# Nodes left in their own order, a written order across engines, and a paced gather stream, in a four-layer graph network

## The chip, the cores and the metric

The kernel runs on one core of a Trainium2 chip. The core has five engines with an instruction queue each: PE (TensorE, matrix products and transposes into PSUM), DVE (VectorE, elementwise work, reductions, sorting steps), ACT (ScalarE, activations and copies), POOL (GpSimd, which here issues indirect DMAs, that is gathers and scatters by a list of row numbers) and SP (SyncE, which issues plain DMAs). They run side by side and wait for each other through semaphores.

The metric is the device time of one execution in microseconds (us). The kernel before took 2909.86 us, the median of 11 runs (2902.86 to 2919.98).

## What is computed

There are 16 graphs of 1024 nodes with 64 features. `adj` is a weighted adjacency matrix with about nine entries per row and the diagonal. Four layers follow each other, each on `h = relu(layernorm(x))` and each added to `x`. The first is a product with `adj` and a weight; the second is a two-layer perceptron, a product with `adj` and a GRU cell; the third is a Chebyshev stack of degree 3, that is two products with `adj`. The fourth needs the work that the change is about:

```python
adj_ = jnp.where(eye[None], 1.0, adj)                 # the node itself counts
nb = (adj_ > 0) & (~eye)[None]
m = nb.sum(-1)
skip = jnp.where(m > 10, (m + 1) // 2, 1)             # nodes with over 10 neighbours
removed = nb & do_dil & ((rank + 1) % skip == 0)      # drop every skip-th neighbour
valid = where(removed | removed.T, 0, adj_) > 0
sv = sort(where(valid, x[neighbour], big), axis=neighbour)
agg = sum over (0.25, 0.5, 0.75) of weight * interpolated quantile of sv, per feature
y = relu((x + agg) @ W1 + b1) @ W2 + b2
```

So for every node and every feature the values of the node and its kept neighbours are sorted, and quantiles of the sorted values are mixed.

## The kernel before, in words

**Lists.** Per graph, `lists` loads eight row tiles of the adjacency (128 x 1024 numbers, L340). DVE turns each into keys (L342), finds the neighbours' keys with MAX8 and MATCH_REPLACE8 (L345 to L350) and writes up to 24 neighbour numbers per node, the count and the two dropped neighbours into `pay`, a row of everything that is known of a node. PE transposes the same row tiles (L356), ACT copies them out of PSUM (L357) into `AT`, which the three matrix layers use.

**Layers.** `layers` runs the first three layers of one graph as one chain: layer norm (DVE L450 and L451, ACT L455, L457 and L463), products with `AT` (L472), small products (L483), the GRU (L518 to L538). The last norm writes `h` into `pay` (L463); then SP stores `h` and the two dropped neighbours as rows of a DRAM table (L721).

**Classes.** Four graphs make a group of 4096 nodes. `positions` ranks the group's nodes by neighbour count, and 32 scatters on POOL (L318) write their `pay` rows to DRAM in that order. The sorted nodes are cut into ten classes, `CLASSES = ((1, 25), (3, 13), ..., (5, 6))`: so many tiles of 128 nodes with at most so many values each. `quantile_class` loads a class's rows (L600), and POOL gathers one neighbour for 128 nodes with each instruction (L606). DVE marks dropped neighbours (L611 to L618), adds a large number to them (L621), sorts by min and max over two buffers (L663, L665) and weighs the sorted places (L673). PE sums them (L680) and computes the perceptron (L689 to L700), DVE finishes the result (L703, L705), and POOL scatters it to `out`, a scatter for each tile (L318).

**Order.** `run` issues, for each graph of a group, the lists, the layers, the store and a quarter of the ten classes of the group before. After the last group its ten classes follow alone. Each engine keeps its queue's order. The tables' unused halves are filled once with large numbers by 64 stores from ACT (L301).

Of the kernel before, what the change touches and what calls it, by code (L numbers as in the profile page):

```python
# [22 lines left out]
P = 128  # L23
# [13 lines left out]
GG = 4  # L37
GT = GG * NT
LIST = 24
BINS = LIST + 1  # L40
FAR = 2000.0
STRIDE = 2 * N
# [3 lines left out]
for _n in (1, 1, 1, 1, LIST, C, 2, C):  # L46
    ROW.append(ROW[-1] + _n)
SELF, TO, COUNT, MASK, IDX, H, DROPS, XS, W = ROW

CLASSES = ((1, 25), (3, 13), (3, 11), (3, 11), (4, 10), (2, 9), (3, 9), (4, 8), (4, 7), (5, 6))  # L50
BIG = 1e30

# [103 lines left out]
def fast_constants():  # L156
# [6 lines left out]
        "bins": np.broadcast_to((BINS - 1 - np.arange(BINS))[None, :], (P, BINS)),  # L163
        "ordinal": np.broadcast_to(1 + np.arange(LIST)[None, :], (P, LIST)),
    }
    kmax = max(n for _, n in CLASSES)
    cap = np.array([n for tiles, n in CLASSES for _ in range(tiles)])
# [4 lines left out]
        "shift": np.broadcast_to(P * np.arange(NT)[None, :], (P, NT)),  # L172
        "place": np.broadcast_to(np.arange(kmax)[None, :], (P, kmax)),
        "taus": np.broadcast_to(np.array([TAUS[0], TAUS[1], TAUS[1], TAUS[2]])[None, :], (P, 4)),

        "room": np.broadcast_to(P * np.array([(cap - 1 >= BINS - 1 - b).sum() for b in range(BINS)])[None, :],
                                (P, BINS)),
    }
# [8 lines left out]
    return tables  # L187


class Fast:  # L190
# [4 lines left out]
    def __init__(self, tc, half, whole, weights):  # L195
# [19 lines left out]
        self.ones16 = fixed("ones16", [P, GT * BINS], F16)  # L215
# [7 lines left out]

        self.aug = fixed("aug", [C + 1, N], F32)
        nc.vector.memset(self.aug[C:C + 1, :], 1.0)

        with tc.tile_pool(name="fsetup", bufs=1) as sp, \
# [12 lines left out]
            self.w2a = fixed("w2a", [C + 1, C], F32)  # L240
            nc.sync.dma_start(self.w2a[:C, :], W2)
            nc.sync.dma_start(self.w2a[C:C + 1, :], b2[None, :])
            self.wca = fixed("wca", [C + 1, C], F32)
            nc.sync.dma_start(self.wca[:C, :], Wc)
            nc.sync.dma_start(self.wca[C:C + 1, :], bc[None, :])
# [35 lines left out]
            tmax = max(t for t, _ in CLASSES)  # L281
            self.mb2r = fixed("mb2r", [1, tmax, C], F32)
            nc.sync.dma_start(self.mb2r, mb2[None, None, :].to_broadcast([1, tmax, C]))

        self.p1 = pool("f1", 1)
        self.p2 = pool("f2", 2)
        self.p3 = pool("f3", 3)
        self.pp = pool("fpay", GG + 2)
        self.ps = pool("fps", 1, space=PSUM)
        self.ps2 = pool("fps2", 2, space=PSUM)  # L290
        self.ps3 = pool("fps3", 3, space=PSUM)
        self.pd = pool("fd", 2, space=DRAM)
        void = self.p1.tile([P, C + 2], F32, name="void")
        nc.vector.memset(void, BIG)
        fixed_d = pool("fdconst", 1, space=DRAM)
        self.tables = []
        for i in range(2):
            table = fixed_d.tile([GG * STRIDE, C + 2], F32, name=f"table{i}")
            for s in range(GG * 2 * NT):
                if s // NT % 2:  # L300
                    nc.scalar.dma_start(table[s * P:(s + 1) * P, :], void)  # L301
            self.tables.append(table)
        self.overs = 0
        self.written = []

    def feature_bank(self, rows=C):
        return self.ps3.tile([P, 512], F32, name="fm")[0:rows, :]

    def after(self, ins, earlier):

        self.tc.add_manual_dep(ins.ins, earlier.ins.name,
                               mybir.DependencyInfo(mybir.DependencyClass.Sync, mybir.DependencyReason.DATA),
                               reason="rows of a scatter")

    def scatter(self, out, rows, at, done):


        ins = self.nc.gpsimd.indirect_dma_start(  # L318
            out=out, out_offset=bass.IndirectOffsetOnAxis(ap=at, axis=0), in_=rows, in_offset=None)
        if done:  # L320
            self.tc.declare_no_dep(ins.ins, done[-1].ins, reason="rows of their own")
        done.append(ins)
# [6 lines left out]
    def lists(self, b, g, adj, nodemask, pay, d):  # L329
# [3 lines left out]
        nc, p1, p2 = self.nc, self.p1, self.p2  # L333
        halves = [self.p3.tile([P, NT, 512], F32, name="AT") for _ in range(2)]
        cand = p2.tile([P, NT, NB], F16, name="cand")
        L = p2.tile([P, NT, LIST], F16, name="L")
        sums = p2.tile([P, NT], F32, name="sums")
        for t in range(NT):
            A = self.p2.tile([P, N], F32, name="A")
            nc.sync.dma_start(A, adj[b, t * P:(t + 1) * P, :])  # L340
            key = p2.tile([P, N], F16, name="key")
            nc.vector.scalar_tensor_tensor(key, A, 0.0, self.keys[:, (NT - 1 - t) * P:(NT - 1 - t) * P + N],  # L342
                                           op0=ALU.is_gt, op1=ALU.mult, accum_out=sums[:, t:t + 1])
            for s in range(NT):
                nc.vector.max(out=cand[:, t, 8 * s:8 * s + 8], in_=key[:, s * P:(s + 1) * P])  # L345
            for s in range(LIST // 8):
                top = L[:, t, 8 * s:8 * s + 8]
                nc.vector.max(out=top, in_=cand[:, t, :])
                if s < LIST // 8 - 1:
                    nc.vector.match_replace(out=cand[:, t, :], in_to_replace=top,  # L350
                                            in_values=cand[:, t, :], imm_value=0.0)
            for h in range(2):
                tp = self.ps2.tile([P, 4, P], F32, name="tp")
                for q in range(4):
                    j = 4 * h + q
                    nc.tensor.transpose(tp[:, q, :], A[:, j * P:(j + 1) * P], self.ident)  # L356
                nc.scalar.activation(halves[t // 4][:, 4 * h:4 * h + 4, (t % 4) * P:(t % 4 + 1) * P], tp, AF.Copy)  # L357

        mu8 = p1.tile([NT, P], U8, name="mu8")
        nc.sync.dma_start(mu8, nodemask[b, :].rearrange("(t p) -> t p", p=P))  # L360
        mf = p1.tile([NT, P], F32, name="mf")
        nc.vector.tensor_copy(mf, mu8)
        mps = self.ps.tile([P, NT], F32, name="mps", tag="nm")
        nc.tensor.transpose(mps, mf, self.ident[:NT, :NT])
        nc.vector.tensor_copy(pay[:, :, MASK], mps)
        nc.vector.tensor_scalar(pay[:, :, SELF], self.node, float(b * N), None, op0=ALU.add)
        nc.vector.tensor_scalar(pay[:, :, TO].bitcast(I32), self.node, float(b * N), None, op0=ALU.add)

        def small(name, n=1):
            return p2.tile([P, NT, n] if n > 1 else [P, NT], F32, name=name)  # L370

        def wide(name, n=1):
            return p1.tile([P, NT, n, LIST] if n > 1 else [P, NT, LIST], F16, name=name)

        some = wide("some")
        nc.vector.tensor_scalar(some, L, 0.0, None, op0=ALU.is_gt)
        cnt = small("cnt")
        nc.vector.tensor_reduce(cnt, some, axis=AX.X, op=ALU.add)
        found = small("found")
        nc.vector.tensor_reduce(found, L, axis=AX.X, op=ALU.add)  # L380
        nc.vector.tensor_sub(found, sums, found)
        nc.vector.tensor_reduce(self.over_column(), found, axis=AX.X, op=ALU.max)

        skip = small("skip")
        nc.vector.tensor_scalar(skip, cnt, 0.5, 0.25, op0=ALU.mult, op1=ALU.add)
        nc.vector.tensor_scalar(skip, skip, MAGIC, MAGIC, op0=ALU.add, op1=ALU.subtract)
        dil = small("dil")
        nc.vector.scalar_tensor_tensor(dil, cnt, 10.0, pay[:, :, MASK], op0=ALU.is_gt, op1=ALU.mult)  # L390
        nc.vector.scalar_tensor_tensor(skip, skip, FAR / 2, dil, op0=ALU.subtract, op1=ALU.mult)
        at = p2.tile([P, NT, 3], F16, name="at3")
        nc.vector.tensor_scalar(at[:, :, 0], skip, FAR / 2, None, op0=ALU.add)
        nc.vector.tensor_scalar(at[:, :, 1], skip, 2.0, FAR, op0=ALU.mult, op1=ALU.add)
        nc.vector.tensor_scalar(at[:, :, 2], skip, 2.0, FAR - 1.0, op0=ALU.mult, op1=ALU.add)
        hit = wide("hit", 3)
        for i in range(3):
            nc.vector.tensor_tensor(hit[:, :, i, :], self.ordinal[:, None, :].to_broadcast([P, NT, LIST]),
                                    at[:, :, i:i + 1].to_broadcast([P, NT, LIST]), op=ALU.is_equal)
# [33 lines left out]
    def layers(self, b, x, halves, pay):  # L433
# [6 lines left out]
        def nodes(name):  # L440
            return p2.tile([P, NT, C], F32, name=name)
# [153 lines left out]
    def quantile_class(self, s0, T, n, rows, placed, table, out):  # L595
# [5 lines left out]
        for ins in placed:  # L601
            self.after(load, ins)
# [763 lines left out]
```

## Time and profile before

| | |
|---|---|
| median of 11 runs | 2909.86 us |
| the profiled execution | 2905.68 us |
| its span in the profile | 2903.9 us |
| mean granted PE clock | 0.683 |
| gathers L606: instructions, busy, mean | 1092, 1150.8 us, 1054 ns |
| scatters to rows L318: instructions, busy, mean | 128, 147.7 us, 1154 ns |
| scatters to out L318: instructions, busy, mean | 128, 162.3 us, 1268 ns |
| a gather's issue to landing, min / median / max | 2.3 / 2.5 / 6.6 us |
| key L342: instructions, busy | 128, 154.6 us |
| sort L665 and L663, the three largest groups, busy | 362.5, 215.5, 53.8 us |
| mask L621, weigh L673, busy | 78.9, 85.0 us |
| product passes with AT, L472 | 2048, busy 559.2 us |
| last gather starts, span ends | 2855.9, 2903.9 us |

The span is the time from the first to the last recorded instruction; the run is a little longer. The page of the profile gives each engine's busy time, a strip of 40 slices with the busy share in tenths, and groups of instructions by line and tile. The view of the waits says, for each engine and line, for whom it stood idle and for how long. The timeline lists instructions with start, duration, engine, line, operation and tiles, and in brackets the idle time before them. The windows give busy time for stretches of the span. An instruction on POOL here is the issue of a DMA: its duration is the time POOL needs to describe 128 row transfers, and the data land later. Durations of DVE instructions that follow each other overlap a little, so the time from start to start is shorter than the mean duration.

### The profile page before, as it was taken

The numbers are of one execution on the slowest core, as the hardware profiler recorded it, in microseconds if no ns is written. First come the engines' busy times: TensorE is split into PE (matmuls) and PEld (weight loads), VectorE is DVE, ScalarE is ACT, GpSimd is POOL, SyncE is SP. The second block draws the span as 40 slices with busy tenths as digits, with TensorE's granted clock in tenths as the row PEclk, the third lists the DMA queues.
The fourth block names the chain that finished last, engine by engine and source line by source line (L and its number), as shares of the span: only waits on it lengthen the run. The fifth ranks groups of instructions, "written<-read, shape, count | busy, mean of one in ns | idle before, by whom it ended". The sixth has DMA issues, their size and how long they took to land. (4 is left out here: it accounts for less than half of the span.)

```text
span 2903.9 us, 22669 instructions
## 1 busy us (share of the span) xinstructions
PE 1484.4 (51%) x6173; PEld 789.9 (27%) x6173; DVE 1547.7 (53%) x5020; ACT 807.3 (28%) x2410; POOL 1461.0 (50%) x1352
## 2 busy tenths in 40 slices
PE   2676766556466574656546646575566412121122
PEld 1333233233223232333213232343232202010111
DVE  4555255475756663676657372667564414544342
ACT  2344354242323242424214232333333100000000
POOL 0000004753644557727546657645646776565764
PEclk9777777667667576767666766676787655555555
DMA  4122012130303131302113131303111111111110
GB/s 123 37 66 66 17 49 96 32 86 16 89 16 89 21 91 44 85 20 67 45 20 92 25 92 42 90 16 87 24 31 32 41 39 23 25 28 21 30 31 16
DMA packets 125605, 142.18 MB, mean 49 GB/s; under 512 B 68766, under 2 KB 87390, under 8 KB 125470
## 3 DMA queue, kind: packets, MB, share of 16 engines
q1 hardware_dynamic: 54142, 82.05, 9.2%
q0 software_dynamic: 45184, 51.54, 8.8%
q10 hardware_dynamic: 26144, 7.07, 1.1%
q8 instruction: 51, 0.84, 0.1%
q14 instruction: 84, 0.69, 0.1%
HBM read 119.51 MB, written 21.04 MB: 48 GB/s over the span
## 5 line engine op out<-in xcount | busy, mean ns | idle before, releaser
L606 POOL DMA_INDIRECT G<-table,PS x1092 | 1150.8, 1054 | 493.9 <-issue 325.4
L680 PE MATMUL q<-buf,c 128*128 128x192 f32 (+4 forms) x696 | 204.2, 464 | 636.3 <-DVE buf L673 636.1
L318 POOL DMA_INDIRECT rows<-pay,at x128 | 147.7, 1154 | 511.3 <-ACT sq L455 469.1
L318 POOL DMA_INDIRECT out<-yo,PS x128 | 162.3, 1268 | 428.0 <-DVE yo L705 303.4
L665 DVE TENSOR_TENSOR buf<-buf 128x576 f32<-128x576 f32 (+11 forms) x552 | 362.5, 681 | 5.1 <-ACT buf L620 0.5
L472 PE MATMUL fm<-AT,h 128*64 128x512 f32 x1024 | 277.2, 694 | 153.6 <-ACT h L463 153.4
L680 PEld LDWEIGHTS q<-buf,c 128*128 128x128 f32 x696 | 162.6, 279 | 681.1 <-DVE buf L673 602.3
L611 DVE TENSOR_TENSOR hits<-G,PS 128x48 f32<-128x48 f32 (+5 forms) x40 | 8.7, 216 | 632.3 <-DMA G<-table,PS 627.3
L472 PE MATMUL fm<-AT,m 128*64 128x512 f32 x1024 | 282.0, 698 | 44.2 <-DVE m L550 37.4
L356 PE MATMUL tp<-c,A 128*128 128x128 f32 x1024 | 205.8, 364 | 178.4 <-DMA A<-in_adj 94.3
L345 DVE MAX8 cand<-key 128x8 f16<-128x128 f16 x1024 | 224.7, 273 | 0.1
L356 PEld LDWEIGHTS tp<-c,A 128*128 128x128 f32 x1024 | 163.5, 189 | 224.9 <-ACT AT L357 106.6
L357 ACT ACTIVATE AT<-tp 128x512 f32<-128x512 f32 x256 | 146.6, 592 | 260.2 <-PE fm L472 110.8
L665 DVE TENSOR_TENSOR buf<-buf,buf 128x384 f32<-128x384 f32 (+9 forms) x460 | 215.5, 497 | 2.3
L455 ACT ACTIVATE sq<-X,st 128x64 f32<-128x64 f32 x384 | 128.2, 336 | 247.9 <-DVE st L451 246.8
L342 DVE SCALAR_TENSOR_TENSOR key<-A,c 128x1024 f16<-128x1024 f32 x128 | 154.6, 1208 | 43.1 <-DMA A<-in_adj 43.0
L472 PEld LDWEIGHTS fm<-AT,h 128*64 128x64 f32 x1024 | 80.8, 160 | 324.7 <-ACT h L463 191.1
L635 ACT ACTIVATE off<-off 128x108 f32<-128x108 f32 (+8 forms) x40 | 11.3, 282 | 545.5 <-DVE off L632 545.5
L463 ACT ACTIVATE h<-X,noff,ri 128x64 f32<-128x64 f32 x384 | 132.5, 427 | 95.5 <-DVE noff L461 95.5
L523 DVE SCALAR_TENSOR_TENSOR of_h<-fm,bhn,nz 64x512 f32<-64x512 f32 x32 | 23.8, 744 | 251.8 <-ACT nz L519 154.0
L503 PE MATMUL fm<-c,h 128*64 128x128 f32 x128 | 42.6, 422 | 204.9 <-ACT h L463 204.8
L472 PEld LDWEIGHTS fm<-AT,m 128*64 128x64 f32 x1024 | 82.6, 161 | 219.0 <-issue 168.5
(155 smaller groups left out, 2167.7 us busy)
## 6 DMA issues: line engine op xcount, KB each, us to landing
A<-in_adj SPq DMA_DIRECT2D x128, 512.0 KB
G<-table,PS POOLq DMA_INDIRECT x1092, 2.5
table<-pay SPq DMA_DIRECT2D x16, 264.0 KB
X<-in_x ACTq DMA_DIRECT2D x16, 256.0 KB
PS<-rows SPq DMA_DIRECT2D x16, 237.0 KB
PS<-rows SPq DMA_DIRECT2D x12, 316.0 KB
table<-void ACTq DMA_DIRECT2D x64, 33.0 KB
rows<-pay,at POOLq DMA_INDIRECT x128, 2.4
```

Source lines behind the costliest of these rows:

```text
L318: ins = self.nc.gpsimd.indirect_dma_start(out=out, out_offset=bass.IndirectOffsetOnAxis(ap=at, axis=0), in_=rows, in_offset=None)
L342: nc.vector.scalar_tensor_tensor(key, A, 0.0, self.keys[:, (NT - 1 - t) * P:(NT - 1 - t) * P + N], op0=ALU.is_gt, op1=ALU.mult, accum_out= ...
L345: nc.vector.max(out=cand[:, t, 8 * s:8 * s + 8], in_=key[:, s * P:(s + 1) * P])
L356: nc.tensor.transpose(tp[:, q, :], A[:, j * P:(j + 1) * P], self.ident)
L357: nc.scalar.activation(halves[t // 4][:, 4 * h:4 * h + 4, (t % 4) * P:(t % 4 + 1) * P], tp, AF.Copy)
L455: nc.scalar.activation(sq, X[:, t, :], AF.Square, bias=st[:, t:t + 1], accum_out=va[:, t:t + 1])
L463: nc.scalar.activation(h[:, t, :], X[:, t, :], AF.Relu, bias=off[:, t:t + 1], scale=ri[:, t:t + 1])
L472: nc.tensor.matmul(o, h[:, j, :], at[:, j, :], start=j == 0, stop=last is None and j == NT - 1)
L503: nc.tensor.transpose(fm[:, t * P:(t + 1) * P], h[:, 4 * half + t, :], ident)
L606: nc.gpsimd.indirect_dma_start(out=G[:, k, t, :], out_offset=None, in_=table, in_offset=bass.IndirectOffsetOnAxis(ap=PS[:, t, IDX + k:IDX ...
L665: nc.vector.tensor_tensor(aps[2], aps[0], aps[1], op=f)
L680: nc.tensor.matmul(zn, self.quarter, bufs[where[k]][:, k, :], start=False, stop=k == places - 1)
```

## The change

Most of the fast path is rewritten. What it computes is the same.

**Nodes stay in place.** There is no group and no ranking of all nodes. Every node of a graph gets ten gathers, so a graph is one class of 8 tiles with 11 values (`NEAR = 11`), whose result one plain store writes to `out`. Only nodes with over 10 kept neighbours are done once more after the last graph: `longest` numbers them over all graphs, and `MANY = ((1, 23), (2, 15), (6, 13))` gives them nine tiles. Their rows come by 9 row gathers from `rows` in DRAM, their results go by 9 scatters over those of the plain stores. Missing neighbours point at one row of large numbers per graph.

**Searched sort.** For 11 and 13 values `NETWORKS` lists min and max steps with first cell and stride of each operand, 28 and 39 instructions; the other two sizes keep the network of before. The gathers' 66-column rows are sorted as they are, in two buffers `G` and `net`.

**Woven order.** All work is given by generators (`listing`, `transposing`, two of `layering`, `gathering`, `quantiling`, `dense`), one operation at a time. `Weave.run` gives each operation a modelled cost (a gather 1.33 us and 2.2 until it has landed), keeps a clock for each engine, and next issues the operation that can start first, within 0.1 us by a key that follows the graph's number. The order on each engine is fixed by added dependencies. Buffers come from stocks (two of `G`, one of `net`, four of `pay`, 15 of `AT`). Where the model leaves PE idle for over 0.5 us, 0.9 of the gap is filled with matmuls whose result is not used.

**Two loads of the adjacency.** Lists load row tiles as before; `transposing` loads column blocks (128 columns, 512-byte pieces) of its own and feeds PE from these. X loads move from ACT's queue to SP's.

**Paced gathers.** Every sixth gather waits until the one before the last has landed:

```diff
+PACE = (6, 2)
...
+    def gather(self, out, table, at, reads):
+        self.count += 1
+        after = self.recent[-PACE[1]:][:1] if PACE and self.count % PACE[0] == 0 else ()
+
+        def make():
+            ins = self.nc.gpsimd.indirect_dma_start(
+                out=out, out_offset=None, in_=table, in_offset=bass.IndirectOffsetOnAxis(ap=at, axis=0))
+            for earlier in after:
+                self.weave.after(ins, earlier)
+            self.recent = self.recent[-2:] + [ins]
+            return ins
+        return Op(self.G, make, [out], [reads, at], 1.33, 2.2, after)
```

The rest of the diff, cut to what the prediction speaks of:

```diff
-CLASSES = ((1, 25), (3, 13), (3, 11), (3, 11), (4, 10), (2, 9), (3, 9), (4, 8), (4, 7), (5, 6))
+NEAR = 11
+MANY = ((1, 23), (2, 15), (6, 13))
+NETWORKS = {
+    11: (
+        ("min", 5, (5, 1), (0, 1), (11, 1)), ("max", 5, (5, 1), (0, 1), (5, 1)),
...
+SLACK = 0.1
+FILL = 0.9
...
+            line = min(best, key=best.get)
+            chain = min((c for c in heads if c["op"].line is line and c["start"] <= best[line] + SLACK),
+                        key=lambda c: c["key"])
+            op, start = chain["op"], chain["start"]
+            if self.spare and line is self.spare[0]:
+                gap = start - self.free.get(line, 0.0)
+                for _ in range(int(FILL * gap / self.spare[4]) if gap > 0.5 else 0):
+                    self.issue(Op(line, self.spare[1], *self.spare[2:4], self.spare[4]), self.free.get(line, 0.0), ("spare", 0))
...
+        weave.spare = (self.T, lambda: nc.tensor.matmul(busy, ones[:, 0:P], ones[:, 0:512], start=True, stop=True),
+                       [busy], [ones], 0.22)
...
+        for t in weave.stocks["G"]:
+            nc.vector.memset(t, 0.0)
+        void = weave.stocks["net"][0]
         nc.vector.memset(void, BIG)
...
+        nc.gpsimd.dma_start(self.table.rearrange("(g s) c -> g s c", s=STRIDE)[:, N, :], void[0:GRAPHS, 0:R])
...
+    def transposing(self, adj):
...
+            yield D.dma_start(block, adj[b, :, j * P:(j + 1) * P].rearrange("(t p) m -> p t m", p=P))
...
+    def gathering(self):
+        for b in range(GRAPHS):
+            yield float(b) + 1.0
+            yield lambda: b in self.paid
+            c = dict(T=NT, n=NEAR, PS=self.paid[b], key=float(b) + 1.0, graph=b)
+            yield from self.gathers(c, ("table", b, b + 1, 0, 1))
+        key = float(GRAPHS) + 1.0
+        yield key
+        yield lambda: hasattr(self, "whom")
+        s0 = 0
+        for T, n in MANY:
+            whole = yield "pay"
+            PS = whole[:, 0:T, :]
+            for t in range(T):
+                yield self.gather(PS[:, t, :], self.rows, self.whom[:, s0 + t:s0 + t + 1],
+                                  ("rows", 0, GRAPHS, 0, 1))
...
+    def gathers(self, c, reads):
+        T, n, PS = c["T"], c["n"], c["PS"]
+        c["G"] = whole = yield "G"
+        G = c["cells"] = whole[:, 0:n * T * R].rearrange("p (k t c) -> p k t c", t=T, c=R)
+        for k in range(n - 1):
+            for t in range(T):
+                yield self.gather(G[:, k + 1, t, :], self.table[0:reads[2] * STRIDE, :], PS[:, t, IDX + k:IDX + k + 1].bitcast(I32),
+                                  reads)
+        self.gathered.append(c)
...
+            for op, k, *sides in NETWORKS[n]:
+                a, b, o = (bufs[st // n][:, st % n:st % n + (k - 1) * step + 1:step, :] for st, step in sides)
+                yield V.tensor_tensor(o, a, b, op=getattr(ALU, op))
```

## The prediction

> **What bounds the kernel now.** First the page: span, busy shares and the strip of 40 slices.
>
> ```profile
> span 2903.9 us, 22669 instructions
> PE 1484.4 (51%) x6173; PEld 789.9 (27%) x6173; DVE 1547.7 (53%) x5020; ACT 807.3 (28%) x2410; POOL 1461.0 (50%) x1352
> DVE  4555255475756663676657372667564414544342
> POOL 0000004753644557727546657645646776565764
> PEclk9777777667667576767666766676787655555555
> ```
>
> No engine is full. POOL does nothing for six slices of 72.6 us, and from slice 33 on POOL and DVE work alone. Second, the waits of POOL and DVE, longest in total first:
>
> ```profile
> DVE hits L611 <- DMA G<-table,PS: 627.3, 39, 63.4
> ...
> POOL rows L318 <- ACT sq L455: 469.1, 4, 468.2
> POOL G L606 <- issue: 325.4, 1026, 7.5
> POOL out L318 <- DVE yo L705: 303.4, 14, 40.2
> POOL G L606 <- DMA PS<-rows: 157.8, 31, 7.9
> ```
>
> POOL's first work waits 468 us for four graphs to be laid out; later it stands behind output scatters (303 us) and row loads (158), while DVE waits 627 us for gathers. The two take turns: the bound is their order. Third, POOL's timeline, and DVE's at the same time:
>
> ```profile
> 2373.11 0.94 POOL L606 DMA_INDIRECT G<-table,PS  x1 [0.30 <-issue]
> 2374.36 0.94 POOL L606 DMA_INDIRECT G<-table,PS  x1 [0.30 <-issue]
> 2375.61 2.23 POOL L606 DMA_INDIRECT G<-table,PS  x1 [0.30 <-issue]
> 2378.14 0.96 POOL L606 DMA_INDIRECT G<-table,PS  x1 [0.30 <-issue]
> ```
>
> ```profile
> 2375.20 1.81 DVE L621 SCALAR_TENSOR_TENSOR buf<-bad,G 128x1600 f32<-128x1600 f32 x1
> 2376.93 0.16 DVE L618 TENSOR_TENSOR m<-PS,m 128x5 f32<-128x5 f32 x1
> 2377.12 2.23 DVE L665 TENSOR_TENSOR buf<-buf 128x960 f32<-128x960 f32 x2
> ```
>
> A gather costs 0.94 us plus 0.30 between two, 1.25, until DVE runs large instructions with two tensor inputs; then one takes 2.23. I laid DVE's timeline over all of POOL's: 40 unbroken runs hold 1,291 of its 1,348 gathers and scatters in 1,776 us. Together these exceed 0.944 us each by 164 us, and DVE spent 497 of the 1,776 us in two-input instructions (sort L663/L665, weighing L673, masking L621, key L342): 0.33 us of stretch per us. In pieces of eight gathers the pitch is 1.26 where such work fills under 5%, 1.35 at 5 to 20%, and 1.47 to 1.55 in all classes above.
>
> **The change, part by part.** I expect POOL to become the bound, so the sum runs along it.
>
> *Lead, 145 us.* Nodes stay in place, so a graph's gathers need its own layers alone. Graph 0's table store is issued at 170.3 now, after ACT sat 36.3 us behind the 64 filler stores (the wait of AT L357 on table<-void), which become one POOL DMA: 134. Added: DVE clears 14,784 columns first, 13 us at the 0.91 us of the 1,024-column clear L225, of which 6 already pass in weight loads, and a landing of about 3. Bounds: 120 if the two woven graphs do not delay each other, 190 if adjacency, now read by row (lists) and by 512-byte block (transposes), fills the queue: the first 100 us now run at 115 GB/s, and twice graph 0's 4 MB takes 73 us at that rate.
>
> *POOL's instructions, 1774 us.* 16 graphs x 8 tiles x 10 = 1,280 gathers; the long rows 1x22 + 2x14 + 6x12 = 122, with 9 row gathers and 9 scatters: 1,420, against 1,348 now, at 1.249. Gone are 119 of 128 output scatters, and all 128 row scatters; 16 row and 16 output stores go to SP instead (0.38 us of its queue each, as table<-pay; the next graph's gathers need only its table store, which is why a store's landing stands in the lead). SP's queue also takes the 128 block loads and ACT's 16 loads of x: some 340 issues at 0.4 are 136 us of it. A load that waits there for a buffer holds back the stores behind it; two graphs laid out ahead cover that, and without the cover it is a seam.
>
> *Stretch, 300 us.* The sort for 11 has 28 instructions over 66 cells of 528 numbers. From the rows 128x320 (482 ns) and 128x960 (1156 ns) a number costs 1.05 ns, and two of 768 take 1.82 us back to back, so 0.1 fixed: 39.5 us a graph, 16 graphs 632, the long rows 78: 710, now 632 (362.5 + 215.5 + 53.8). Weighing scales with its numbers to 108 (85.0 x 1.27), masking to 101 (78.9 x 1.28), key stays 154.6: 1,074, of which some 70 fall before the first or after the last gather. 1,005 x 0.33 = 332; by the pieces, at a share near half but unevenly spread, a pitch of 1.45, 284. I take 300. Bounds: 160 (0.16, what a fit gives for instructions under 0.7 us) and 710 (0.71, what a fit by overlap gives for L621's, 1.2 to 2.6 us long; the new sort has many of 1.1 to 2.8).
>
> The Trainium skill (SBUF — State Buffer, Who interferes with whom) says a DVE instruction with two SBUF inputs holds the shared read port for its whole length against GpSimd reads, yet infers that a tensor_tensor leaves descriptor generation alone. By that inference this term would be 0 and the sum 2,056; the 2.23 us row beside L621 and L665 speaks against it.
>
> *The wait, 45 us.* 1,411 gathers give 235 waits on the landing of the last but one. A landing comes 2.5 us after the gather's start (median of the tile's view, 2.3 to 6.6), and two pitches are 2.5: usually nothing is left. Over 260 triples of the trace the landing would have held the third back by 0.19 us in the mean (0 for three quarters, 0.55 at the 90th of 100): 235 x 0.19 = 45. Bounds 0 and 130 (0.55 each). Behind it on POOL stand all later gathers; DVE waits for the last of 80.
>
> *Seams, 15 us.* Three row gathers must land (2.5 us each) before their long rows; two G buffers give POOL a graph of 80 gathers, some 117 us, to have the last sorted. Bounds 0 and 60.
>
> *Tail, 77 us.* The last class: 1.8 us to DVE as at 2374.6, 0.6 small, 4.9 masking, 38 sort, 4 weighing, about 7.5 for 22 matmul passes (0.57 each at half clock now, ten in 5.7), 10 dense, 2.2 landing, 0.4 flag and 7.9 after it as now. Its six scatters are in POOL's count.
>
> *Off the path.* The adjacency is read twice: 67 MB more, by packets like those of the software queue (51.5 MB for 8.8% of 16 engines) 11.5% more, beside 19% now; its price, if it delays gathers, is in the wait's upper bound. DVE grows to 1548 + 78 + 23 + 22, with the long-row numbering and extra copies about 1,715: 73% of the new span. If POOL ran freely it would set the end near 1,950. ACT's 807 hardly changes; up to 64 more table loads at 1.28 us are 82. PE's 1484 is at a mean clock of 0.683. The fill matmuls are in no row: 0.2 to 0.64 us each, the latter as a 64x512 pass of L525. The order inserts them only into modelled gaps, so I put them at nothing: 1484 x 0.683 = 1,014 us of work at full clock leaves 1,300. That cover goes if the clock stays low (rival 3).
>
> Sum: 145 + 1774 + 300 + 45 + 15 + 77 = 2,356 us of span. The profiled run took 2905.68 around 2903.9, and the median is 4 higher: 2,362, say **2360**.
>
> **Rivals.**
> 1. *Little stretch.* If gathers and sort fall apart in the woven order, stretch is 100 and the wait 10: about 2,125. For: 70 of 143 pieces of eight gathers have under 5% of such work beside them. Against: DVE must be three quarters busy in the same time.
> 2. *The order strands engines.* It is fixed from modelled costs (1.33 us a gather, against my 1.45); when gathers come late, DVE stands before a sort with layer work queued behind it. At 20 us a graph, as POOL's waits for yo cost now (303 us in 14 waits), 16 x 20 = 320: 2,680. Against: two graphs are layered ahead, four pay buffers.
> 3. *PE stays at half clock.* The trace's clock records are 0.5 for 1,843 us, else 1.0. The order is some 2,000 us long in its own costs (1,420 x 1.33, and the lead), so fills of 0.9 of the gaps beside 1,014 us of work are about 900 us. At half clock fills and work would need 3,800; a clock that is half for a third of the time, as an estimate, makes 1,914 x 1.33 = 2,550, and with lead and seams 2,700. The Trainium skill (TensorE: Matmul & The Clock Gate, Part 1) says about 3.4 us of sustained work opens the clock; by that, fills prevent this, and the sum stands.
> 4. *Slower: POOL shut out.* If every us of two-input work holds POOL back fully, stretch is 1,005 and the time 3,065. It passes 2,910 from 0.85 us per us. For: 2.23 us gathers beside L621. Against: 0.33 over the trace, no class above a pitch of 1.55.
> 5. *The wait never holds*, as the landing is always earlier: 2,315, inside my range.
>
> **How the numbers follow.** Forecast 0.55 (own range 2200 to 2500), rival 1 0.15, rival 2 0.15, rival 3 0.04, rival 4 0.06, rival 5 0.05. Low 2120 takes in rival 1; high 2640 most of the stretch's upper bound and half of rival 2. A measurement of this kernel tells some 0.2% from no change. Faster 0.92: all but rival 4 and the ends of 2 and 3; same 0.01; slower 0.07.
>
> **What would show it.** First gather near 145; POOL without a gap between graphs and a mean gather of 1.1 to 1.25 us; DVE near 1,715; granted clock over 0.9; paced gathers 0.2 us later than others. Wrong if POOL shows idle stretches of over 10 us a graph, if DVE waits for PE, or if the mean gather passes 1.5.

## The result and the profile after

The changed kernel takes 2636.91 us (median of 8 runs, 2626.94 to 2643.31). Its ratio to the kernel before is 0.9056, 95% interval 0.9041 to 0.9071: 273 us less, where the forecast of 2360 had 550 less. The profiled execution's span is 2637.5 us, mean granted clock 0.883. The page, its busy shares and strips of 40 slices (65.9 us each now):

```profile
span 2637.5 us, 29044 instructions
PE 2318.7 (88%) x9635; PEld 1034.2 (39%) x9635; DVE 1829.8 (69%) x4162; ACT 879.4 (33%) x2351; POOL 1729.4 (66%) x1425
...
DVE  6768897869795958777876868686728474548334
...
POOL 0037667777777767677677677767777777777740
PEclk8999998888898988887989888988879899798997
```

The holes are gone: POOL works at 6 or 7 tenths from the first gather to the last, and 7 is nearly all it can show, since 0.94 us of work and 0.30 us between two gathers make 0.76. PE looks full, but 857 us of its 2,319 are fills (L538, 3,658 matmuls). Line numbers in the trace are those of a helper (L285) for most work; the tile names tell it apart. The waits of POOL, longest in total first (total us, times, longest):

```profile
POOL G L590 <- issue: 367.8, 1170, 4.0
POOL G L590 <- DMA G<-table,pay: 270.0, 196, 8.3
POOL G L590 <- DVE L L285: 141.2, 1, 141.2
```

The third line is the lead, a single wait (what it waits for is said under the lead below). The first is the ordinary 0.3 us between two gathers. The second is what the pacing brings: 196 waits for a gather's landing, where the kernel before had 10.7 us of them in all. POOL's timeline shows where they fall (start, duration, and in brackets the idle time before it and what ended it):

```profile
1104.40 0.94 POOL L590 DMA_INDIRECT G<-table,pay  x1 [0.30 <-issue]
1106.10 0.94 POOL L590 DMA_INDIRECT G<-table,pay  x1 [0.76 <-DMA G<-table,pay]
...
1114.07 0.94 POOL L590 DMA_INDIRECT G<-table,pay  x1 [0.79 <-DMA G<-table,pay]
...
1122.34 0.94 POOL L590 DMA_INDIRECT G<-table,pay  x1 [1.07 <-DMA G<-table,pay]
```

Each sixth gather starts 0.46 to 0.77 us late, in a quiet stretch where every gather takes 0.94 us. The second loss stands 100 us earlier, POOL above and DVE below:

```profile
996.85 0.94 POOL L590 DMA_INDIRECT G<-table,pay  x1 [0.30 <-issue]
998.09 5.48 POOL L590 DMA_INDIRECT G<-table,pay  x1 [0.30 <-issue]
1003.87 3.50 POOL L590 DMA_INDIRECT G<-table,pay  x1 [0.30 <-issue]
```

```profile
997.27 5.49 DVE L285 SCALAR_TENSOR_TENSOR G<-bad,G 128x5120 f32<-128x5120 f32 x1
...
1003.65 2.90 DVE L285 TENSOR_TENSOR net<-G 128x2640 f32<-128x2640 f32 x1
```

A gather that starts beside the masking instruction of 5.49 us takes 5.48 us instead of 0.94 and ends 0.8 us after it (997.27 + 5.49 = 1002.76, 998.09 + 5.48 = 1003.57). The next ends 0.8 us after the sort's first instruction.

**One account for every run.** POOL's timeline splits each span without a rest: the start of the first gather; 1,411 gathers at 1.249 us (0.944 and the 0.305 to the next, 1,762 us); what they last beyond 0.944 us (*stretch*); what the gaps before paced gathers exceed 0.305 us (*wait*); the same for all other gaps (*seams*); and the time after the last gather (*tail*). Changed kernel: 167.7 + 1,762 + 387.8 + 222.8 + 7.2 + 89.9 = 2,637.

### The profile page after: what moved, and what is told of

It is laid out like the page before. It is cut to its first block, busy times and chain, and to the rows that moved or that the text cites. A ratio compares the mean times of both kernels' runs of the same rounds, so it can differ in the third digit from the quotient of the medians.

```text
span 2637.5 us, 29044 instructions
## 1 busy us (share of the span) xinstructions
PE 2318.7 (88%) x9635; PEld 1034.2 (39%) x9635; DVE 1829.8 (69%) x4162; ACT 879.4 (33%) x2351; POOL 1729.4 (66%) x1425
## 5 line engine op out<-in xcount | busy, mean ns | idle before, releaser
L590 POOL DMA_INDIRECT G<-table,pay x1402 | 1709.3, 1219 | 794.7 <-issue 367.8
L538 PE MATMUL bank<-ones 128*128 128x512 f16 x3658 | 856.8, 388 | 0.4 <-DVE wg L503 0.4
L285 PE MATMUL bank<-AT,nodes 128*64 128x512 f32 x2048 | 627.0, 678 | 87.1 <-DVE nodes L285 58.5
L538 PEld LDWEIGHTS <-ones 128*128 128x128 f16 x3658 | 357.8, 100 | 454.5 <-issue 82.4
L285 PEld LDWEIGHTS bank<-AT,nodes 128*64 128x64 f32 x2048 | 164.1, 153 | 422.7 <-issue 265.4
L285 ACT ACTIVATE sq<-pay,st 128x64 f32<-128x64 f32 x512 | 177.5, 347 | 174.7 <-DVE st L285 160.9
L285 ACT ACTIVATE AT<-bank 128x512 f32<-128x512 f32 x256 | 145.3, 592 | 244.6 <-PE bank L285 243.7
L285 PE MATMUL bank<-c,block 128*128 128x128 f32 x1024 | 173.3, 304 | 55.4 <-DMA block<-in_adj 43.8
L285 PE MATMUL bank<-G,c 128*128 128x512 f32 (+3 forms) x362 | 156.1, 570 | 74.5 <-DVE G L285 73.3
L285 DVE MAX8 cand<-key 128x8 f16<-128x128 f16 x1024 | 213.5, 279 | 3.8
L285 DVE TENSOR_TENSOR hits<-G,pay 128x160 f32<-128x160 f32 (+3 forms) x19 | 5.9, 312 | 297.0 <-DMA G<-table,pay 296.7
L285 ACT ACTIVATE wide<-bank 64x512 f32<-64x512 f32 x128 | 75.5, 590 | 394.9 <-PE bank L285 393.9
L285 PEld LDWEIGHTS bank<-c,block 128*128 128x128 f32 x1024 | 130.0, 155 | 162.5 <-issue 131.9
L285 DVE TENSOR_TENSOR G<-G 128x528 f32<-128x528 f32 (+6 forms) x138 | 187.3, 1358 | 3.4
L285 DVE SCALAR_TENSOR_TENSOR key<-row,c 128x1024 f16<-128x1024 f32 x128 | 154.8, 1209 | 10.4 <-DMA row<-in_adj 10.4
L285 ACT ACTIVATE nodes<-pay,off,ri 128x64 f32<-128x64 f32 x384 | 141.7, 429 | 34.5 <-DVE off L285 34.3
L285 ACT ACTIVATE off<-off 128x288 f32<-128x288 f32 (+3 forms) x38 | 16.1, 423 | 388.9 <-DVE off L285 388.3
L285 DVE TENSOR_TENSOR net<-G 128x1056 f32<-128x1056 f32 (+9 forms) x103 | 140.8, 1383 | 1.0
L285 PE MATMUL bank<-wide,wg 64*64 64x512 f32 (+1 forms) x192 | 114.8, 701 | 19.2 <-ACT wide L285 19.1
L285 DVE TENSOR_TENSOR yo<-bank,pay 128x256 f32<-128x256 f32 (+2 forms) x36 | 14.7, 408 | 164.8 <-PE bank L285 158.2
L285 PEld LDWEIGHTS bank<-G,c 128*128 128x128 f32 x362 | 63.2, 199 | 133.0 <-issue 66.0
L285 DVE TENSOR_TENSOR G<-net 128x1056 f32<-128x1056 f32 (+9 forms) x86 | 109.2, 1309 | 1.3
```

What stands on the lines that cost most here:

```text
L285: return Op(self, lambda: f(*args, **kwargs), writes, reads, cost, later)
L538: weave.spare = (self.T, lambda: nc.tensor.matmul(busy, ones[:, 0:P], ones[:, 0:512], start=True, stop=True), [busy], [ones], 0.22)
L590: ins = self.nc.gpsimd.indirect_dma_start(out=out, out_offset=None, in_=table, in_offset=bass.IndirectOffsetOnAxis(ap=at, axis=0))
```

## The experiments

The theory: POOL's stream of gathers sets the end, so each us that is taken out of its wait or stretch comes off the time. The rivals: the time is set by the order or by PE and DVE, and POOL's losses would only move elsewhere.

**The wait out, the order kept** (time 2509.75 us, ratio 0.8622, 0.8587 to 0.8656):

```diff
-            for earlier in after:
-                self.weave.after(ins, earlier)
```

> The 235 waits are taken out; the written order is still made as if they were there, so that every engine keeps its order. In the changed kernel the gaps before the paced gathers are 223 us longer than the usual 0.3 us, 0.95 each. Theory A (POOL is the bound and the wait is simply lost time on it): the gaps go, a sixth of them comes back as longer gathers beside the sort, and the time is 2637 - 190 = about 2450 us. Rival B (the gathers are then held by something else, a full DMA queue or DVE): POOL's gathers grow by as much as the gaps shrink, or POOL idles elsewhere, and the time stays above 2590.

**The wait out, and the order made without it** (2430.90 us, 0.8345, 0.8309 to 0.8380):

```diff
-PACE = (6, 2)
+PACE = None
```

> No waits, and the order is made without them too. Theory A: as with the wait taken out in the same order, about 2450 us, within 30 us of that run. If the order made for paced gathers is what matters, the two differ by more than 50 us.

**The wait one gather further back** (2522.63 us, 0.8660, 0.8629 to 0.8691):

```diff
-PACE = (6, 2)
+PACE = (6, 3)
```

> Every sixth gather waits for the landing of the last but two in place of the last but one, a gather (1.25 to 1.6 us) more time for it to land. Theory A, with a landing that is late by some 0.5 us from the landing to the start of the waiting gather, and by more where the adjacency is loaded: the mean extra gap falls from 0.95 us to about 0.25, and the time to about 2637 - 150 = 2490 us. If a wait costs the same whatever has landed (a restart of POOL's queue), the gaps stay near 0.9 us and the time near 2630.

With the order made anew, the wait falls from 223 us to 1, the seams grow from 7 to 31, and the time falls by 206 us. In the kept order only 127 us are won, as the seams grow to 121. I had expected some 2450 us of both, within 30 us of each other; they are 79 apart, so the order counts too. The waits of POOL in the kernel with the kept order name its seams:

```profile
POOL G L590 <- DVE net L285: 111.3, 8, 17.0
```

POOL reaches the end of a graph's 80 gathers sooner than the order was made for, and waits for DVE to finish sorting the `G` buffer that it needs next: 8 waits, 17.0 us the longest. One gather further back leaves 114 us of wait, 0.49 us at each where I had expected 0.25, though 1.25 us more are given: two thirds of the paced gathers (158 of 235) lose nothing then, but a tenth lose 2 us or more (POOL's timeline). So what is still paid for there is a tail of late landings, not a fixed delay.

**Sort, masking and weighing in shorter pieces, the wait kept** (2505.57 us, 0.8608, 0.8570 to 0.8646). Masking and weighing are cut to 16 rows of 64 numbers, the sort to two cells an instruction:

```diff
-                a, b, o = (bufs[st // n][:, st % n:st % n + (k - 1) * step + 1:step, :] for st, step in sides)
-                yield V.tensor_tensor(o, a, b, op=getattr(ALU, op))
+                for i in range(0, k, 2):
+                    m = min(2, k - i)
+                    a, b, o = (bufs[st // n][:, st % n + i * step:st % n + (i + m - 1) * step + 1:step, :]
+                               for st, step in sides)
+                    yield V.tensor_tensor(o, a, b, op=getattr(ALU, op))
```

> The waits stay; DVE's long two-input instructions (mask and weighing of 1,408 to 5,120 numbers, sorting steps of 3 and 5 cells) are cut into pieces of at most 1,056 numbers, the same numbers in all, some 20 instructions more a graph (32 us of DVE in all). In the changed kernel 99 gathers beside two-input instructions of 2 us and more hold 214 of the 388 us of stretch. If a gather is held until the DVE instruction that runs has ended: stretch falls by about 150 us, and the time to about 2500. Rival: the stretch goes by the time that two-input work takes, 0.33 us per us whatever its pieces: stretch stays near 390 and the time is 2637 or a little more.

The stretch falls from 388 to 255 us, the time by 131, with the same numbers sorted and DVE's busy time even 16 us longer (1845.4). The masking of another graph in the timeline, POOL and then DVE:

```profile
819.39 1.61 POOL L590 DMA_INDIRECT G<-table,pay  x1 [0.30 <-issue]
...
823.81 1.67 POOL L590 DMA_INDIRECT G<-table,pay  x1 [0.30 <-issue]
825.78 1.97 POOL L590 DMA_INDIRECT G<-table,pay  x1 [0.30 <-issue]
```

```profile
818.97 2.35 DVE L285 SCALAR_TENSOR_TENSOR G<-bad,G 128x1024 f32<-128x1024 f32 x2
...
823.44 3.49 DVE L285 SCALAR_TENSOR_TENSOR G<-bad,G 128x1024 f32<-128x1024 f32 x3
```

Beside the same masking in pieces of some 1.2 us, gathers take 1.6 to 2.0 us and not 5.5. The first ends at 821.00, 0.8 us after the end of the first of two pieces (818.97 + 1.18), while the second is still running. So a gather waits for the end of the instruction it meets and then gets on, though the next one follows at once: the length of one instruction decides, and not the sum of them.

DVE's being busy is not enough. In the changed kernel 348 gathers into `G` start while a DVE instruction with both inputs in SBUF has 0.3 us or more to go, and 336 of them end 0.8 us after it. Another 42 start in the same way beside an instruction with one input in SBUF (a reduction, or the other input in PSUM): all take 0.95 us or less. And a gather that is already under way isn't held: 72 had none beside them at their start and such a two-input instruction begin within their first 0.6 us, and none of them took over 0.95 us.

**The adjacency's column blocks loaded twice in all** (2577.45 us, 0.8845, 0.8805 to 0.8884):

```diff
-            yield D.dma_start(block, adj[b, :, j * P:(j + 1) * P].rearrange("(t p) m -> p t m", p=P))
+            if i < 2:
+                yield D.dma_start(block, adj[b, :, j * P:(j + 1) * P].rearrange("(t p) m -> p t m", p=P))
```

> Leaves out 126 of the 128 column-block loads (PE transposes stale blocks, so the three matrix layers of all but the first two blocks get wrong adjacency); row loads, gathers and the wait stay. In the changed kernel a paced gather waits 1.1 to 1.5 us more than usual while both loads run and 0.33 in the last 240 us, where none does. If the landing is late because of the loads' traffic: the mean extra gap falls from 0.95 to about 0.5 and the time by some 100 to about 2535 us. If a wait costs POOL a fixed restart: the gap stays at 0.95 and the time near 2630.

**Nearly no adjacency load at all, the wait kept** (2518.69 us, 0.8642, 0.8609 to 0.8676). As the one above, and of the row tiles only tile 2 of graph 10 and tile 3 of graph 4 are loaded:

```diff
-            yield D.dma_start(row, adj[b, t * P:(t + 1) * P, :])
+            if b == 0 and t < 2:
+                g, i = ((10, 2), (4, 3))[t]
+                yield D.dma_start(row, adj[g, i * P:(i + 1) * P, :])
```

> The paced gathers stay; nearly all adjacency loads are left out: each of the two block buffers and of the two row buffers is loaded once, and the transposes and the lists work on what lies there, so the neighbours taken are others. Gathers, sort and order of the rest stay as they are. Leaving out the blocks alone took the mean loss at a paced gather from 0.95 to 0.72 us. If adjacency traffic is what makes landings late, the mean loss falls to the 0.3 us that the changed kernel shows after its loads have ended: 235 x 0.65 = 150 us less than the changed kernel, about 2485. If the landing is late through the gathers' own descriptors or the read of the table, it stays near 0.7 and the time near 2570.

The loss at a paced gather goes with the traffic: 0.95, 0.72 and 0.48 us in the mean, for 187.5, 121.5 and 55.4 MB read. The DMA part of the page, first the changed kernel, then the last one (packets, MB, share of the 16 engines):

```profile
q1 hardware_dynamic: 220156, 157.56, 22.2%
...
HBM read 187.51 MB, written 19.17 MB: 78 GB/s over the span
```

```profile
q0 software_dynamic: 45616, 48.49, 13.5%
q1 hardware_dynamic: 70972, 25.42, 5.3%
...
HBM read 55.39 MB, written 19.17 MB: 30 GB/s over the span
```

The adjacency's loads make half of the wait, 110 of 223 us (with a reservation: the lists made from stale tiles make the gathers of the last kernel read other rows of the table). I had expected more of both steps (0.5 us without the blocks, 0.3 without any). The other half stays with some 50 MB of the gathers' queue and 25 MB of other loads left. The median loss there is 0.22 us, the mean 0.48; what makes the late ones among them is open.

**No fills** (`FILL = 0.0`, 2639.10 us, 0.9054, 0.9021 to 0.9088):

> The paced kernel without the fill matmuls (3,658 of them, 857 us of PE in the changed kernel). My forecast put them at nothing, as PE is not on the path: clock from 0.88 to about 0.7, PE's other work from 1,460 to some 1,700 us busy, and the time within 30 us of 2637. Rival: fills stand in front of layer work on PE's queue (ACT waits 515 us for PE's banks): faster by 30 or more. Second rival: the full clock is needed: slower by 60 or more.

```profile
PE 1721.3 (65%) x5977; PEld 761.2 (29%) x5977; DVE 1828.8 (69%) x4162; ACT 881.9 (33%) x2351; POOL 1727.4 (65%) x1425
...
PEclk9769788777676777677777676777766765555555
```

3,658 matmuls fewer, a mean granted clock of 0.706 instead of 0.883, and the time is the same: PE has slack at either clock here. The Trainium skill (TensorE: Matmul & The Clock Gate, Part 1) says that an idle PE falls to half clock; the row of fives at the end agrees. It is a rule on PE's speed, and a bound elsewhere makes it worth nothing.

**Both losses taken away**: no wait and the pieces of above (2398.64 us, 0.8245, 0.8210 to 0.8280), and no wait with pieces of one cell, or 8 rows (2372.58 us, 0.8164, 0.8132 to 0.8196; the loop's lines are against the pieces of above):

```diff
-PACE = (6, 2)
+PACE = None
...
-                for i in range(0, k, 2):
-                    m = min(2, k - i)
+                for i in range(0, k, 1):
+                    m = min(1, k - i)
```

> No wait, and long two-input instructions cut to at most 1,056 numbers. The two effects were 206 us (no wait) and 131 us (pieces), on different terms, POOL's gaps and POOL's gathers. If they add: 2637 - 206 - 131 = 2300 us. If another engine becomes the bound (DVE, 1846 us busy with pieces, and its waits for PE of some 200): above 2360.

> No wait, and every sorting step, mask and weighing cut to at most 528 numbers: 38 sorting steps, 8 masks and 7 weighings more a graph, at 0.1 us each 85 to 95 us more of DVE in all than uncut. If a gather is held to the end of the DVE instruction that runs, pieces half as long halve the stretch again, 255 to about 140, and the time is about 2300 - 110 + what DVE's 1,920 us cost it: 2200 to 2260. If back-to-back pieces hold POOL like one instruction from here on: stretch stays near 250 and the time is 2300 or more.

The mechanism holds on: at one cell the stretch is 127 us, the mean gather 1.03 us. Of these 127 us, 47 fall on gathers held by the key instruction, 1.21 us long and not cut, and 29 on five gathers that no DVE instruction beside them explains. But the two effects do not add: the times are 99 and over 110 us above what I expected of them, for the seams grew as the stretch fell: 31, 122, 222 us. POOL's group and its waits with one-cell pieces:

```profile
L590 POOL DMA_INDIRECT G<-table,pay x1402 | 1448.8, 1033 | 781.5 <-issue 396.4
```

```profile
POOL G L590 <- DVE ri L285: 141.9, 1, 141.9
...
POOL G L590 <- DMA table<-pay: 71.4, 4, 22.6
POOL G L590 <- DVE cand L285: 34.1, 1, 34.1
POOL G L590 <- DVE net L285: 31.9, 4, 17.2
```

The first is the lead again. The rest are new, and the engine that a line names is only the last that signalled. The wait of 34.1 us that is put down to `cand`, a tile of the lists, ends like this:

```profile
980.77 0.38 SPq L600 DMA_DIRECT2D table<-pay  x1
...
986.09 0.94 POOL L590 DMA_INDIRECT G<-table,pay  x1 [34.12 <-DVE cand L285]
```

The store of this graph's table was issued only 5.3 us before. It is the same at the first gather of each graph from 7 to 15: it starts 4.7 to 6.4 us after its own table store (once 10.2), and PE had read out the buffer it fills 14 us or more before. These nine waits are 162 of the 222 us. Graphs 4 and 5 wait for DVE's sort, whose step ends 0.3 us before. Of the 254 us that shorter pieces took out of the stretch, 191 came back as seams.

**What holds it there.** Three kernels on the one-cell version: a gather priced 1.20 us in the written order instead of 1.33 (2376.92 us, 0.8157, 0.8134 to 0.8180), priced 1.45 (2457.91 us, 0.8429, 0.8405 to 0.8453), and no fills (2434.21 us, 0.8358, 0.8339 to 0.8377):

```diff
-        return Op(self.G, make, [out], [reads, at], 1.33, 2.2, after)
+        return Op(self.G, make, [out], [reads, at], 1.2, 2.2, after)
```

> No paced gathers, sort, masking and weighing in one-cell pieces as in the 2373 us kernel, and the written order made with 1.20 us for a gather instead of 1.33. There POOL loses 222 us in waits for DVE and for table stores. If that loss comes from an order made for slower gathers, it falls below 120 and the time to about 2270. If the loss comes because DVE and PE cannot deliver sooner, the time stays within 2350 to 2400.

> As the 2373 us kernel, with 1.45 us for a gather in the written order instead of 1.33. If the order's price decides, the loss of 222 us grows or falls by some 50 us against the kernel priced 1.33, opposite in sign to the one priced 1.20; if DVE and PE are the bound, both stay within 2350 to 2400.

> No paced gathers, one-cell pieces, and no fill matmuls. With POOL no longer the only bound, PE's pace may reach the end now: if DVE's and POOL's waits hang on PE, the lower clock makes it slower than 2373, about 2450 or more; if fills stand in PE's way, it gets faster, about 2330; if PE still has slack, it stays within 20 us of 2373.

The cheaper price changes nothing; the seams are 256 us and the stretch 101. The dearer one gives 85 us away, which neither of my two cases for it had. So an order made for slower gathers isn't what holds the one-cell version up; a still slower one hurts. Without fills (clock 0.741) the seams grow from 222 to 300 us and the time by 62: here PE's pace counts, as it did not while POOL was the bound. The table stores say what the limit at 2,373 is. From graph 7 to 15 they come every 125 us at the price of 1.33, every 126 at 1.20 and every 130 without fills, while POOL needs some 105 to 110 us for a graph's gathers: the layers deliver graphs more slowly than POOL takes them. Which engine's work inside the layers sets this pace was not separated.

## Why the prediction was off

That the time falls and that POOL becomes the bound was right: taking 222 us of wait or 133 us of stretch out of POOL's stream took 206 and 131 us off the time. The size was wrong by 277 us, inside the wide range (2120 to 2640), outside the likeliest case's own (2200 to 2500). Term by term:

| term of the sum | predicted | measured |
|---|---|---|
| lead, first gather | 145 | 167.7 |
| POOL's instructions | 1774 | 1762, and 11 of scatters in the tail |
| stretch | 300 | 388 |
| wait | 45 | 223 |
| seams | 15 | 7 |
| tail without its scatters | 77 | 79 |
| span | 2356 | 2637 |

**The step that failed is "The wait, 45 us"**, its mean of 0.19 us at each of 235 gathers. It is 0.95 us, outside the bounds of 0 to 130 us too. The price came from 260 triples of the trace before, and left out two things.

First, it let the third gather start at the landing itself; in the kernel without the column blocks the trace records 48 of the awaited landings, and the waiting gather starts 0.26 us after each. In the changed kernel only one waiting gather starts earlier than 1.64 us after the end of the gather it waits for (1.58), and half of them later than 2.2, where 1.55 us are there for nothing (0.305 + 0.944 + 0.305). Even after the last loads, past 2,300 us, the loss is 0.33 us. With 0.26 us added the old triples would have given some 0.35 us in the mean, an estimate.

Second, landings of a kernel with half the adjacency traffic were taken for the new one's: the loss is 1.1 to 1.5 us up to 1,600 us of the span, while loads run, and without them it is halved (0.48). The doubled traffic is not all of it: with the column blocks left out the kernel reads 121 MB, as the kernel before did (120), and the loss is still 0.72. Of the landings that the traces record, those of the kernel before come 1.69 us after the gather's end in the mean, and those of this one 2.11; why they are later at the same volume stays open. I had put that traffic "in the wait's upper bound", but that bound was the 90th of 100 of the same old triples, so it held no new traffic at all. The rival that the wait never holds pointed the wrong way.

**The stretch** was mis-sized by 88 us. The rate of 0.33 us per us that I read off the trace came out (388 us beside 1,165 us of two-input work), but I went below it to 300, and the work was 1,165 us, not 1,005: some 180 us of it are short instructions, under 0.7 us, in layers and lists, that I had left out and that stretch little (6 us). The other 986 us carry the rest, 0.39 us per us, most of it beside the longest: 99 gathers beside an instruction of 2 us and more carry 214 of the 388 us. A price per us of work missed that length decides; the row 2.23 us beside L621 had already shown it. The inference of the Trainium skill (SBUF — State Buffer, Who interferes with whom) that a `tensor_tensor` leaves descriptor generation alone does not make this term 0: a gather takes 3.50 us beside a `tensor_tensor` of 2.90. But a gather also reads its row numbers from `pay` in SBUF, and no run tells whether that reading is held or the writing of descriptors. The Trainium skill's rule that the port is held for an instruction's whole length agrees with the pieces.

**The lead** was 23 us longer, within its bounds. The waits name DVE's `L`, a tile of the lists, but by the times it was what the prediction had: graph 0's table store, issued at 162.5 where the prediction has 141, and landing after some 5 us instead of 3:

```profile
162.53 0.39 SPq L600 DMA_DIRECT2D table<-pay  x1
...
167.69 1.01 POOL L590 DMA_INDIRECT G<-table,pay  x1 [141.19 <-DVE L L285]
```

With nearly no adjacency loads the two are at 156.8 and 162.3, so the loads are at most 6 us of it; what else made graph 0's layers late stays open.

**Off the path.** Fills at nothing was right, and shown by leaving them out. The cover behind it is POOL's being the bound, and once that goes they are worth 62 us. The clock of over 0.9 was not reached (0.883) and did not matter. DVE was busy 1,830 us, not 1,715. "POOL without a gap between graphs" was right with 7 us of seams.

**The rivals.** Little stretch: no, it was more. The order strands engines: not in the changed kernel, but 111 us of it appeared as soon as the wait was taken out of its order. PE at half clock: no; it was at 0.883, and at 0.706 the time was the same. POOL shut out: no, at 0.33 us per us.

## What to carry to other kernels

Price a wait on a DMA's landing from the traffic of the new kernel, with the time from landing to start added, and by the mean with its late ones (0.95 us here, where the median is 0.47); on the engine that is the bound, nearly each us of it is a us of the end. Where POOL issues many small gathers beside DVE's elementwise work, cut long two-input instructions: at one cell a piece the same work cost the gathers a third of the stretch (127 for 388 us), and 47 us of that stand beside the one long instruction that was left whole. And remove the bound's losses one at a time: of the first 222 us 206 reached the time, of the next 254 only some 60, as the layers of the next graph were not ready. Look up the times before believing the engine that a wait is put down to: two of the waits above were named after the wrong one.

## What the runs showed of the hardware

A gather that starts while a DVE instruction with both inputs in SBUF runs stands still until that one ends, and is done some 0.8 us later: 0.94 us alone, 1.6 to 2.0 beside pieces of 1.2 us, 5.48 beside one of 5.49. One that starts before the instruction is not held. Pieces of some 0.65 us, back to back, leave it at 0.94 to 1.4 us, as the one-cell version shows, POOL and then DVE:

```profile
565.49 0.98 POOL L590 DMA_INDIRECT G<-table,pay  x1 [0.30 <-issue]
566.77 1.21 POOL L590 DMA_INDIRECT G<-table,pay  x1 [0.30 <-issue]
```

```profile
566.49 1.89 DVE L285 SCALAR_TENSOR_TENSOR G<-bad,G 128x512 f32<-128x512 f32 x3
```

Unexpected as well was how far a landing is moved by other loads: the same gathers lose 0.33 us at a wait when nothing else is loaded and 1.1 to 1.5 us while 512 KB loads run, with the 16 DMA engines busy for 43% of the time.
